# Layer 1 of a four-layer convolution stack: a 3x3 convolution computed by pairs of rows

## The chip, the cores and the metric

The kernel runs on one core of a Trainium2 chip. The metric is the device time of one execution in microseconds; the time before is the median of three runs. A profile is one further execution, recorded by the hardware profiler. TensorE (PE) multiplies matrices and writes to PSUM, VectorE (DVE) and ScalarE (ACT) work element by element on SBUF and PSUM, GpSimd (POOL) here clears borders and issues the stores, and SyncE (SP) issues the loads. Each engine works through its own list of instructions in order and waits on semaphores for the others.

## What is computed

The input x has the shape (4, 64, 256, 256): four images (batches) of 64 channels, all in float32. Four layers follow one another, each of the form x = x + f(groupnorm(x)), with 32 groups of two channels. Cut to what matters here:

```python
x = x + _L0_conv_ref(_gn(x), ...)      # 1x1, 8x8 patch filter, depthwise 3x3, gelu gate, 1x1
x = x + _L1_conv_ref(_gn(x), kernel)   # this layer
x = x + _L2_conv_ref(_gn(x), ...)      # masked periphery
x = x + _L3_conv_ref(_gn(x), ...)      # spectral layer

def _L1_conv_ref(x, kernel):           # kernel: (64, 64, 3, 3)
    return jax.lax.conv_general_dilated(x, kernel, window_strides=(1, 1),
        padding=[(1, 1), (1, 1)], dimension_numbers=('NCHW', 'OIHW', 'NCHW'))
```

So layer 1 is a dense 3x3 convolution from 64 to 64 channels with a border of zeros, on the normalized input, and the input itself is added to the result (the residual).

## The kernel before

The four layers run one after the other; each keeps its result in DRAM (`x1`, `x2`, `x3`), and the next reads it. Layers 0 and 2 write out the order of the instructions on PE, DVE, ACT and SP by hand (`tc.manual_schedule`); layer 1 before the change leaves the order to the scheduler of the language, which follows the data dependencies and the order of the program text.

Layer 1 (`_layer1`, from L703) works in 64 steps: for each of the 4 batches 16 steps of 16 image rows. In a step the upper 8 rows lie on partitions 0 to 63 (one channel each) and the lower 8 rows on partitions 64 to 127. `halves` are these two ranges.

- `load(n)` fetches a step, one step ahead: the tile `x` with 10 rows per half (8 and one on either side, L724), and, in another arrangement, the tile `xr` with the same 8 rows per half once more (L728). `xr` serves as residual and takes the result.
- `normalize` (L210, called at L748) is one ScalarE instruction that scales and shifts `x` by the group norm's values of the batch and writes `xn`, which is two columns wider; GpSimd clears those two columns (L737), and the outer row at the top and bottom of an image.
- The products are at L755. For two values of `i` (a pair of output rows in each block of four) and the nine taps `k` of the kernel, four matmuls of 64x64 weights with 2 x 256 columns are issued: `s` says which half of the partitions is read, `j` which of two blocks of four rows, and the result of block `j` lands in the half `j` of a PSUM tile `ps[s]`. The nine taps are accumulated in PSUM. That makes 2 x 9 x 4 = 72 matmuls a step. An fp32 matmul leaves two records in the trace.
- For each of the two PSUM tiles VectorE adds the residual (L761) and takes the statistics that the next group norm needs (L762, `bn_stats`).
- GpSimd issues two stores to `x2` (L765).
- After the last step of a batch `group_norm` (L149, its steps at L153 to L175) aggregates the statistics (L158) and turns them into scale and shift of layer 2: two small matmuls (L161, L170), small VectorE operations and a power on GpSimd (L174).

Layer 2 begins by loading its constants on SP (`load`, L138), then its first tiles of `x2` (L832). VectorE operations of other layers that serve below as a price: L454 (layer 0, a product of an SBUF and a PSUM tile of 1024 elements), L968 (layer 2, an addition of two SBUF tiles of 1024 elements), L980 (layer 2, statistics of 512 elements) and, for ScalarE, L950 (layer 2, a copy of 1024 elements from PSUM).

Of the kernel before, what the change touches and what calls it, by code (L numbers as in the profile page):

```python
# [10 lines left out]
F32 = mybir.dt.float32  # L11
U32 = mybir.dt.uint32
AF = mybir.ActivationFunctionType
ALU = mybir.AluOpType
PSUM = bass.MemoryType.PSUM
DRAM = bass.MemoryType.DRAM

C = 64
# [96 lines left out]
class _Net:  # L115
# [93 lines left out]
    def normalize(self, dst, src, n, b, p0=0, p1=128):  # L209
        self.nc.scalar.activation(  # L210
            dst, src, AF.Identity, bias=self.nb[n][p0:p1, b : b + 1], scale=self.r[n][p0:p1, b : b + 1]
        )
# [483 lines left out]

    def layer1(self, src, dst):
        with ExitStack() as ctx:  # L700
            self._layer1(ctx, src, dst)

    def _layer1(self, ctx, src, dst):  # L703
        tc, nc, a, B, H, W = self.tc, self.nc, self.a, self.B, self.H, self.W
        pool = lambda name, bufs, **k: ctx.enter_context(tc.tile_pool(name=name, bufs=bufs, **k))
        cp, p_x, p_n, p_r = pool("l1c", 1), pool("l1x", 3), pool("l1n", 2), pool("l1r", 3)
        ps_o, ps_s = pool("l1po", 6, space=PSUM), pool("l1ps", 1, space=PSUM)
        small = lambda name: ps_s.tile([128, 512], F32, tag="s", name=name)
        W1 = W + 1
        wk = cp.tile([128, 9, C], F32, name="wk")  # L710
        for s in range(2):
            nc.sync.dma_start(wk[s * C : (s + 1) * C], a["k3"].rearrange("c y x o -> c (y x) o"))
        its = [(b, r0) for b in range(B) for r0 in range(0, H, 16)]
        halves = [slice(0, C), slice(C, 128)]
        tiles = [(s, j) for s in range(2) for j in range(2)]
        raws = {}

        def load(n):
            b, r0 = its[n]
            x = p_x.tile([128, 10, W], F32, tag="x", name=f"x1_{n}")  # L720
            for s in range(2):
                top = r0 + 8 * s - 1
                i0, i1 = max(0, -top), min(10, H - top)
                nc.sync.dma_start(x[halves[s], i0:i1], src[b][:, top + i0 : top + i1, :])  # L724
            xr = p_r.tile([128, 2, 4, W], F32, tag="xr", name=f"xr1_{n}")
            v = src[b][:, r0 : r0 + 16, :].rearrange("c (s j r) w -> j c s r w", s=2, j=2)
            for j in range(2):
                nc.sync.dma_start(xr[halves[j]], v[j])  # L728
            raws[n] = x, xr

        load(0)
        for n, (b, r0) in enumerate(its):
            if n + 1 < len(its):
                load(n + 1)
            x, xr = raws.pop(n)
            xn = p_n.tile([128, 10, W + 2], F32, tag="xn", name=f"xn1_{n}")
            nc.gpsimd.memset(xn[:, :, 0 : W + 2 : W + 1], 0.0)  # L737
            i0, i1 = 0, 10
            if r0 == 0:
                i0 = 1  # L740
                nc.gpsimd.memset(xn[0:C, 0, 1:W1], 0.0)
                self.normalize(xn[C:128, 0, 1:W1], x[C:128, 0], 1, b, C, 128)
                bst = self.stats_tile(f"bst2_{b}", H * W // 1024)
            if r0 + 16 == H:
                i1 = 9
                nc.gpsimd.memset(xn[C:128, 9, 1:W1], 0.0)
                self.normalize(xn[0:C, 9, 1:W1], x[0:C, 9], 1, b, 0, C)
            self.normalize(xn[:, i0:i1, 1:W1], x[:, i0:i1], 1, b)  # L748
            for i in range(0, 4, 2):
                ps = [ps_o.tile([128, 2, W], F32, tag="o", name=f"ps1_{n}_{i}_{s}") for s in range(2)]  # L750
                for k in range(9):
                    dy, dx = divmod(k, 3)
                    for s, j in tiles:
                        r = 4 * j + i + dy
                        nc.tensor.matmul(  # L755
                            ps[s][halves[j]], wk[halves[s], k, :], xn[halves[s], r : r + 2, dx : dx + W],
                            start=(k == 0), stop=(k == 8),
                        )
                for s in range(2):
                    xo = xr[:, s, i : i + 2]  # L760
                    nc.vector.tensor_add(xo, xo, ps[s])  # L761
                    nc.vector.bn_stats(bst[:, r0 // 4 + i + s, :], xo.rearrange("p r w -> p (r w)"))  # L762
            v = dst[b][:, r0 : r0 + 16, :].rearrange("c (s j r) w -> j c s r w", s=2, j=2)
            for j in range(2):
                nc.gpsimd.dma_start(v[j], xr[halves[j]])  # L765
            if r0 + 16 == H:
                self.group_norm(2, b, bst, small)

# [497 lines left out]
```

## Time and profile before

| what | before |
|---|---|
| median of three runs | 7874.6 us |
| the three runs | 7872.5, 7874.6, 7885.55 us |
| the profiled execution | 7916.6 us |
| its span, first to last instruction | 7914.8 us |
| PE busy | 7529.5 us (95%) |
| DVE busy | 6190.4 us (78%) |
| ACT busy | 3598.1 us (45%) |
| POOL busy | 644.5 us (8%) |
| mean granted TensorE clock | 0.969 |
| layer 1, first to last product (4917.3 to 5931.9 us) | 1014.6 us |
| PE, DVE and ACT busy in that stretch | 1005.4, 347.0, 161.4 us |
| DMA share and rate in that stretch | 0.82, 209 GB/s |

A row of the groups gives line, engine, operation, output and inputs with their shapes and the count, then the total busy time in us with the mean time of one in ns, then the time that the engine stood idle just ahead of such instructions and which engine's work ended the wait. Busy times are unions: four matmuls that run at the same time in different parts of the array count once. The windows give busy times of PE, weight loads (PEld), DVE, ACT and POOL in a stretch, with the clock granted to TensorE (1.00 is full speed) and the load on the DMA engines.

### The profile page before, as it was taken

Reading aid. Unit: us, or ns where it says so; the run is one execution under the profiler, and the core shown is the slowest. Engines: PE = TensorE matmul, PEld = TensorE weight load, DVE = VectorE, ACT = ScalarE, POOL = GpSimd, SP = SyncE. Lnnn points to the kernel's source line nnn. Section 1 sums busy time; section 2 is a strip of 40 time slices with the busy share of each in tenths; the row PEclk is TensorE's granted clock in tenths of the full one; section 3 lists DMA queues with packets and bytes.
Section 4 is the critical chain, followed back from the end, with each engine's and each line's share of the span. In section 5 each row is a group of like instructions: output and inputs, shape, how many; then the busy total and the mean of one; then the engine's idle time right before and its main releaser. Section 6 shows DMA issues by size and latency. Waiting matters only on the chain.

```text
span 7914.8 us, 402431 instructions
## 1 busy us (share of the span) xinstructions
PE 7529.5 (95%) x191350; PEld 4403.3 (56%) x191350; DVE 6190.4 (78%) x5653; ACT 3598.1 (45%) x3853; POOL 644.5 (8%) x1465
## 2 busy tenths in 40 slices
PE   5999999999999999999999998999998999997887
PEld 3666666666666666666666665333333444443375
DVE  6999999999999999999989987333337889885345
ACT  2444444444544444444444453111117778774111
POOL 0000000000000000000000000000001222221000
PEclk9999999999999999999999999999999999999955
DMA  5222222222222222221112113888876666667679
GB/s 118 63 61 64 65 58 61 61 60 60 62 60 59 60 62 58 60 61 48 45 45 49 45 48 88 220 214 211 213 185 164 174 176 176 174 175 234 234 301 390
DMA packets 520862, 942.83 MB, mean 119 GB/s; under 512 B 44996, under 2 KB 308116, under 8 KB 501812
## 3 DMA queue, kind: packets, MB, share of 16 engines
q1 hardware_dynamic: 438708, 648.59, 29.9%
q0 software_dynamic: 80512, 268.50, 12.4%
q8 instruction: 1500, 24.58, 1.4%
q14 instruction: 142, 1.16, 0.1%
HBM read 648.48 MB, written 268.44 MB: 116 GB/s over the span
## 4 chain that ended last, share of the span: by engine, by line
PE 88%; DMA 4%; DVE 4%; issue 2%; ACT 1%; SPq 0%; DVEq 0%; ACTq 0%; POOLq 0%; POOL 0%
PE psd L434 30%; PE ps L755 13%; PE psy L407 10%; PE psu L369 8%; PE one L938 7%; PE div L897 5%; PE pso L509 3%; DMA x<-x 3%; PE psz L927 2%; PE psa L1112 2%; PE psF L356 2%; DVE v L472 2%; PE psT L346 2%; PE pso L500 1%; DMA st<-in_x_dram 1%
## 5 line engine op out<-in xcount | busy, mean ns | idle before, releaser
L434 PE MATMUL psd<-y,diag 32*32 32x512 f32 x73296 | 2539.2, 597 | 9.0 <-issue 7.9
L472 DVE SCALAR_TENSOR_TENSOR v<-y,sb_w_dw,v 128x2048 f32<-128x2048 f32 x1024 | 2391.0, 2335 | 108.7 <-ACT v L470 85.9
L434 PEld LDWEIGHTS psd<-y,diag 32*32 32x32 f32 x73296 | 1525.3, 103 | 860.0 <-issue 341.3
L414 ACT COPY y<-psy 128x512 f32<-128x512 f32 x1536 | 915.7, 660 | 1704.4 <-PE psy L407 1702.6
L372 DVE TENSOR_TENSOR up<-psu,flt 128x768 f32<-128x768 f32 x1024 | 932.5, 951 | 238.8 <-PE psu L369 237.8
L407 PEld LDWEIGHTS psy<-sb_c_bdft,up 64*64 64x64 f32 x49152 | 861.3, 135 | 353.2 <-issue 141.9
L755 PE MATMUL ps<-xn,wk 64*64 64x512 f32 x9216 | 1002.8, 592 | 9.7 <-ACT xn L210 9.7
L407 PE MATMUL psy<-sb_c_bdft,up 64*64 64x64 f32 x49152 | 933.1, 221 | 36.5 <-issue 33.7
L210 ACT ACTIVATE xn<-x,nb,r 128x1024 f32<-128x1024 f32 (+3 forms) x272 | 487.8, 1797 | 898.7 <-POOL xn L737 809.7
L369 PE MATMUL psu<-win,xf 64*64 64x384 f32 x8192 | 791.1, 487 | 20.5 <-DVE h L454 10.0
L755 PEld LDWEIGHTS ps<-xn,wk 64*64 64x64 f32 x9216 | 348.8, 133 | 655.3 <-issue 655.2
L761 DVE TENSOR_TENSOR xr<-xr,ps 128x512 f32<-128x512 f32 x256 | 173.7, 679 | 657.8 <-PE ps L755 657.8
L883 DVE TENSOR_TENSOR q<-xn 128x2313 f32<-128x2313 f32 (+2 forms) x256 | 627.7, 2496 | 13.6 <-ACT xn L210 13.6
L938 PE MATMUL one<-z,wp 32*32 32x512 f32 x16384 | 594.4, 596 | 14.0 <-issue 12.1
L884 ACT ACTIVATE q<-q 128x2313 f32<-128x2313 f32 (+2 forms) x256 | 529.0, 2086 | 30.5 <-DVE q L883 29.1
L938 PEld LDWEIGHTS one<-z,wp 32*32 32x32 f32 x16384 | 371.9, 103 | 216.1 <-issue 79.1
L448 ACT ACTIVATE h<-psd 128x1024 f32<-128x1024 f32 x258 | 250.8, 1022 | 527.6 <-PE psd L434 527.5
L897 PE MATMUL div<-q,ones 64*32 64x512 f32 x8192 | 462.8, 596 | 11.4 <-ACT q L884 9.8
L369 PEld LDWEIGHTS psu<-win,xf 64*64 64x64 f32 x8192 | 311.1, 134 | 184.0 <-issue 83.2
L379 POOL MEMSET y<- 128x22 f32 x384 | 51.7, 136 | 4261.3 <-ACT y L387 3225.5
L971 POOL DMA_DIRECT2D x<-r x512 | 271.9, 538 | 978.9 <-DVE r L968 953.4
L897 PEld LDWEIGHTS div<-q,ones 64*32 64x32 f32 x8192 | 152.7, 107 | 314.1 <-issue 244.4
(121 smaller groups left out, 6628.5 us busy)
## 6 DMA issues: line engine op xcount, KB each, us to landing
x<-x SPq DMA_DIRECT2D x240, 640.0 KB, 6.7
x<-x SPq DMA_DIRECT2D x61, 2048.0 KB, 13.4
st<-in_x_dram SPq DMA_DIRECT2D x256, 256.0 KB, 3.6
x<-in_x_dram SPq DMA_DIRECT2D x256, 256.0 KB, 3.8
xr<-x SPq DMA_DIRECT2D x128, 512.0 KB, 5.3
x<-xr POOLq DMA_DIRECT2D x128, 512.0 KB, 6.4
r<-x SPq DMA_DIRECT2D x512, 128.0 KB, 4.1
x<-r POOLq DMA_DIRECT2D x512, 128.0 KB, 4.0
```

What stands on the lines that cost most here:

```text
L210: self.nc.scalar.activation(dst, src, AF.Identity, bias=self.nb[n][p0:p1, b : b + 1], scale=self.r[n][p0:p1, b : b + 1])
L369: nc.tensor.matmul(ps[halves[n], s, 0:384], xf[t][halves[s], n, 4 * g + k], win[halves[s]], start=True, stop=True)
L372: nc.vector.tensor_mul(ups[t, g][:, :, k, :], ps[:, :, 0:384], flt.broadcast_to([128, 2, 384]))
L407: nc.tensor.matmul(ps[halves[c], n, s, :, k, :], up[halves[n], s, k, i * 128 + c * C : i * 128 + (c + 1) * C], bdft[halves[n]], start=True ...
L414: nc.scalar.copy(yt[t][i][:, 3:11, w0 : w0 + 64].rearrange("p r (k n w) -> p n r k w", k=4, n=2), ps[:, :, s])
L434: ins = nc.tensor.matmul(d[q // 2][quarters[j], q % 2], diag[quarters[q], i, k, :], rows_in(t, i, quarters[q], j, dy)[:, :, dx : dx + W], ...
L472: nc.vector.scalar_tensor_tensor(v, s, wdw[:, 2, k : k + 1], v, ALU.mult, ALU.add)
L755: nc.tensor.matmul(ps[s][halves[j]], wk[halves[s], k, :], xn[halves[s], r : r + 2, dx : dx + W], start=(k == 0), stop=(k == 8),)
L883: nc.vector.tensor_sub(d, p0, p1)
L884: nc.scalar.activation(d, d, AF.Square)
L897: ins = nc.tensor.matmul(ps[quarters[j], h], ones[halves[h]], q[n, g, k][halves[h], r + 2 * j : r + 2 * j + 2, o : o + W], start=(m == 0), ...
L938: ins = nc.tensor.matmul(rows2(ps[g])[quarters[j], k], w[quarters[i]], z[quarters[i], h, 2 * j + dy : 2 * j + dy + 2, dx : dx + W], tile_p ...
```

## The change

The convolution is computed by pairs of output rows. For input rows d0 to d3 (normalized, with border) and the three rows w0, w1, w2 of the kernel, a pair of output rows needs d0 w0 + d1 w1 + d2 w2 and d1 w0 + d2 w1 + d3 w2. With the weights g1 = (w0 + w1 + w2) / 2 and g2 = (w0 - w1 + w2) / 2 and the four products

- m0 = (d0 - d2) w0, m1 = (d1 + d2) g1, m2 = (d2 - d1) g2, m3 = (d3 - d1) w2

the pair is m0 + m1 + m2 and m1 - m2 + m3. Each product stands for its three horizontal taps, accumulated in PSUM. The rows of a step form four such pairs per half. So there are 4 x 3 = 12 tap products over all pairs where 2 x 9 = 18 were needed.

The combinations of rows are made by VectorE (`transform`, four instructions of 4 x 258 elements a step). Of the four PSUM tiles (128 x 1024 elements each) m1 is copied to SBUF by ScalarE (`fetch`), m1 + m2 and m1 - m2 are made by VectorE (`middle`), and VectorE adds m0 to the one and m3 to the other (`result`), into a new tile `o`. The residual is accumulated into m0 and m3 by a further product of the raw tile `x` with an identity matrix, so the tile `xr` and its two loads go. Statistics and stores work on `o`. The order on PE, DVE, ACT and SP is now written by hand; loads run three steps ahead, the normalization two, and the steps of the group norm are spread over the following steps of the loop (`next_norms`). The lines of the diff, without the unchanged ends of functions (`load`'s and `normalize`'s bodies stay as they are but for the buffers):

```diff
-        cp, p_x, p_n, p_r = pool("l1c", 1), pool("l1x", 3), pool("l1n", 2), pool("l1r", 3)
-        ps_o, ps_s = pool("l1po", 6, space=PSUM), pool("l1ps", 1, space=PSUM)
+        cp, p_x, p_n, p_t = pool("l1c", 1), pool("l1x", 4), pool("l1n", 1), pool("l1t", 2)
+        p_s, p_o, pp = pool("l1s", 2), pool("l1o", 3), pool("l1p", 1, space=PSUM)
+        def pair(name):
+            return pp.tile([128, 2, 512], F32, tag=f"p{next(turn) % 4}", name=name)
...
+        gs = [wk[:, 0]] + [cp.tile([128, 3, C], F32, name=f"wg{k}") for k in range(2)] + [wk[:, 2]]
+        side = cp.tile([128, 3, C], F32, name="wside")
+        nc.vector.tensor_add(side, wk[:, 0], wk[:, 2])
+        for g, op in ((gs[1], nc.vector.tensor_add), (gs[2], nc.vector.tensor_sub)):
+            op(g, side, wk[:, 1])
+            nc.vector.tensor_scalar(g, g, 0.5, None, ALU.mult)
+        xns = [p_n.tile([128, 10, W + 2], F32, name=f"xn1_{k}") for k in range(2)]
+        for t in xns:
+            nc.gpsimd.memset(t[:, :, 0 : W + 2 : W1], 0.0)
...
-            xr = p_r.tile([128, 2, 4, W], F32, tag="xr", name=f"xr1_{n}")
-            v = src[b][:, r0 : r0 + 16, :].rearrange("c (s j r) w -> j c s r w", s=2, j=2)
-            for j in range(2):
-                nc.sync.dma_start(xr[halves[j]], v[j])
...
-            for i in range(0, 4, 2):
-                ps = [ps_o.tile([128, 2, W], F32, tag="o", name=f"ps1_{n}_{i}_{s}") for s in range(2)]
-                for k in range(9):
-                    dy, dx = divmod(k, 3)
-                    for s, j in tiles:
-                        r = 4 * j + i + dy
-                        nc.tensor.matmul(
-                            ps[s][halves[j]], wk[halves[s], k, :], xn[halves[s], r : r + 2, dx : dx + W],
-                            start=(k == 0), stop=(k == 8),
-                        )
-                for s in range(2):
-                    xo = xr[:, s, i : i + 2]
-                    nc.vector.tensor_add(xo, xo, ps[s])
-                    nc.vector.bn_stats(bst[:, r0 // 4 + i + s, :], xo.rearrange("p r w -> p (r w)"))
...
+        def transform(n, *which):
+            xn = xns[n % 2]
+            if n not in ts:
+                ts[n] = p_t.tile([128, 4, 4, W + 2], F32, tag="t", name=f"t_{n}")
+            d = [xn[:, k : k + 7 : 2] for k in range(4)]
+            for i in which:
+                p, q, op = (
+                    (d[0], d[2], nc.vector.tensor_sub),
+                    (d[1], d[2], nc.vector.tensor_add),
+                    (d[2], d[1], nc.vector.tensor_sub),
+                    (d[3], d[1], nc.vector.tensor_sub),
+                )[i]
+                op(ts[n][:, i], p, q)
+
+        def product(n, i):
+            m = ms[n, i] = pair(f"m{i}_{n}")
+            tiles = [(s, j) for s in range(2) for j in range(2)]
+            for dx in range(3):
+                for s, j in tiles:
+                    nc.tensor.matmul(
+                        rows2(m)[halves[j], s], gs[i][halves[s], dx, :],
+                        ts[n][halves[s], i, 2 * j : 2 * j + 2, dx : dx + W],
+                        start=(dx == 0), stop=(dx == 2 and i in (1, 2)),
+                    )
+            if i in (0, 3):
+                r = 1 if i == 0 else 2
+                for s, j in tiles:
+                    nc.tensor.matmul(
+                        rows2(m)[halves[j], s], self.ident[halves[s], halves[s]],
+                        xt[n][halves[s], r + 4 * j : r + 4 * j + 3 : 2], start=False, stop=True,
+                    )
+
+        def fetch(n):
+            t = sums[n, 1] = p_s.tile([128, 2, 512], F32, tag="s1", name=f"s1_{n}")
+            nc.scalar.copy(t, ms.pop((n, 1)))
+
+        def middle(n):
+            m1, m2 = sums.pop((n, 1)), ms.pop((n, 2))
+            for i, op in ((0, nc.vector.tensor_add), (3, nc.vector.tensor_sub)):
+                t = sums[n, i] = p_s.tile([128, 2, 512], F32, tag=f"s{i}", name=f"s{i}_{n}")
+                op(t, m1, m2)
+
+        def result(n, i):
+            if n not in outs:
+                outs[n] = p_o.tile([128, 2, 4, W], F32, tag="o", name=f"o1_{n}")
+            r = i // 3
+            nc.vector.tensor_add(
+                outs[n][:, :, r : r + 3 : 2], rows2(ms.pop((n, i))), rows2(sums.pop((n, i)))
+            )
+
+        def finish(n):
+            o = outs.pop(n)
+            for s in range(2):
+                for i in (0, 2):
+                    nc.vector.bn_stats(bst[b][:, r0 // 4 + i + s, :], o[:, s, i : i + 2].rearrange("p r w -> p (r w)"))
+            v = dst[b][:, r0 : r0 + 16, :].rearrange("c (s j r) w -> j c s r w", s=2, j=2)
+            for j in range(2):
+                nc.gpsimd.dma_start(v[j], o[halves[j]])
+            if r0 + 16 == H:
+                norms.append(self.group_norm_parts(2, b, bst.pop(b), lambda name: pair(name)[:, 0, :]))
...
+            for n in range(3):
+                load(n)
+            for n in range(2):
+                normalize(n)
+            transform(0, 1, 2, 0, 3)
+            for n in range(NI):
+                load(n + 3)
+                product(n, 1)
+                fetch(n)
+                product(n, 2)
+                finish(n - 1)
+                transform(n + 1, 1, 2)
+                middle(n)
+                product(n, 0)
+                result(n, 0)
+                transform(n + 1, 0, 3)
+                normalize(n + 2)
+                product(n, 3)
+                result(n, 3)
+                next_norms()
+                xt.pop(n)
+                ts.pop(n)
+            finish(NI - 1)
+            while norms:
+                next_norms()
```

More of the change, by code (lines that the diff above doesn't have):

```diff
@@ L705, in _layer1 @@
         pool = lambda name, bufs, **k: ctx.enter_context(tc.tile_pool(name=name, bufs=bufs, **k))
-        cp, p_x, p_n, p_r = pool("l1c", 1), pool("l1x", 3), pool("l1n", 2), pool("l1r", 3)
-        ps_o, ps_s = pool("l1po", 6, space=PSUM), pool("l1ps", 1, space=PSUM)
-        small = lambda name: ps_s.tile([128, 512], F32, tag="s", name=name)
+        cp, p_x, p_n, p_t = pool("l1c", 1), pool("l1x", 4), pool("l1n", 1), pool("l1t", 2)
+        p_s, p_o, pp = pool("l1s", 2), pool("l1o", 3), pool("l1p", 1, space=PSUM)
+        turn = count()
+        def pair(name):
+            return pp.tile([128, 2, 512], F32, tag=f"p{next(turn) % 4}", name=name)
+        rows2 = lambda t: t.rearrange("p s (r w) -> p s r w", r=2)
         W1 = W + 1
-        wk = cp.tile([128, 9, C], F32, name="wk")
+        halves = [slice(0, C), slice(C, 128)]
+        wk = cp.tile([128, 3, 3, C], F32, name="wk")
         for s in range(2):
-            nc.sync.dma_start(wk[s * C : (s + 1) * C], a["k3"].rearrange("c y x o -> c (y x) o"))
+            nc.sync.dma_start(wk[halves[s]], a["k3"])
+        gs = [wk[:, 0]] + [cp.tile([128, 3, C], F32, name=f"wg{k}") for k in range(2)] + [wk[:, 2]]
[7 more added lines that the diff above has]
+            nc.gpsimd.memset(t[:, :, 0 : W + 2 : W1], 0.0)
         its = [(b, r0) for b in range(B) for r0 in range(0, H, 16)]
-        halves = [slice(0, C), slice(C, 128)]
-        tiles = [(s, j) for s in range(2) for j in range(2)]
-        raws = {}
+        NI = len(its)
+        xt, ts, ms, sums, outs, bst, norms = {}, {}, {}, {}, {}, {}, []
         def load(n):
+            if n >= NI:
+                return
             b, r0 = its[n]
-            x = p_x.tile([128, 10, W], F32, tag="x", name=f"x1_{n}")
+            x = xt[n] = p_x.tile([128, 10, W], F32, tag="x", name=f"x1_{n}")
             for s in range(2):
@@ L724, in load, with normalize @@
                 nc.sync.dma_start(x[halves[s], i0:i1], src[b][:, top + i0 : top + i1, :])
-            xr = p_r.tile([128, 2, 4, W], F32, tag="xr", name=f"xr1_{n}")
-            v = src[b][:, r0 : r0 + 16, :].rearrange("c (s j r) w -> j c s r w", s=2, j=2)
-            for j in range(2):
-                nc.sync.dma_start(xr[halves[j]], v[j])
[L729 to L737, printed above, removed]
+        def normalize(n):
+            if n >= NI:
+                return
+            b, r0 = its[n]
+            x, xn = xt[n], xns[n % 2]
             i0, i1 = 0, 10
@@ L742, in _layer1 @@
                 self.normalize(xn[C:128, 0, 1:W1], x[C:128, 0], 1, b, C, 128)
-                bst = self.stats_tile(f"bst2_{b}", H * W // 1024)
             if r0 + 16 == H:
@@ L748, in _layer1 @@
             self.normalize(xn[:, i0:i1, 1:W1], x[:, i0:i1], 1, b)
-            for i in range(0, 4, 2):
-                ps = [ps_o.tile([128, 2, W], F32, tag="o", name=f"ps1_{n}_{i}_{s}") for s in range(2)]
-                for k in range(9):
-                    dy, dx = divmod(k, 3)
-                    for s, j in tiles:
-                        r = 4 * j + i + dy
-                        nc.tensor.matmul(
-                            ps[s][halves[j]], wk[halves[s], k, :], xn[halves[s], r : r + 2, dx : dx + W],
-                            start=(k == 0), stop=(k == 8),
-                        )
-                for s in range(2):
-                    xo = xr[:, s, i : i + 2]
-                    nc.vector.tensor_add(xo, xo, ps[s])
-                    nc.vector.bn_stats(bst[:, r0 // 4 + i + s, :], xo.rearrange("p r w -> p (r w)"))
+        def transform(n, *which):
+            if n >= NI:
+                return
+            xn = xns[n % 2]
[10 more added lines that the diff above has]
+                op(ts[n][:, i], p, q)
@@ L763, in _layer1 @@
+        def finish(n):
+            if n < 0:
+                return
+            b, r0 = its[n]
+            if b not in bst:
+                bst[b] = self.stats_tile(f"bst2_{b}", H * W // 1024)
+            o = outs.pop(n)
+            for s in range(2):
+                for i in (0, 2):
+                    nc.vector.bn_stats(bst[b][:, r0 // 4 + i + s, :], o[:, s, i : i + 2].rearrange("p r w -> p (r w)"))
             v = dst[b][:, r0 : r0 + 16, :].rearrange("c (s j r) w -> j c s r w", s=2, j=2)
@@ L764, in _layer1, with next_norms @@
             for j in range(2):
-                nc.gpsimd.dma_start(v[j], xr[halves[j]])
+                nc.gpsimd.dma_start(v[j], o[halves[j]])
             if r0 + 16 == H:
-                self.group_norm(2, b, bst, small)
+                norms.append(self.group_norm_parts(2, b, bst.pop(b), lambda name: pair(name)[:, 0, :]))
+        def next_norms():
+            for parts in list(norms):
+                if next(parts, self) is self:
+                    norms.remove(parts)
+        with tc.manual_schedule(
+            engines={
+                mybir.EngineType.PE, mybir.EngineType.DVE, mybir.EngineType.Activation, mybir.EngineType.SP
+            }
+        ):
+            for n in range(3):
[23 more added lines that the diff above has]
+                next_norms()
```

## The prediction

> **What bounds the kernel now.** I read the page's slices first, since the change lies in one layer and a share over the whole span mixes four.
>
> ```profile
> PE   5999999999999999999999998999998999997887
> DVE  6999999999999999999989987333337889885345
> PEclk9999999999999999999999999999999999999955
> DMA  5222222222222222221112113888876666667679
> ```
>
> A slice is 197.9 us. Slices 26 to 30 are layer 1: TensorE full, VectorE at three tenths, the DMA engines at eight. Next the groups of instructions there, and the rows that price the new operations (line, engine, operation, names, shapes, count | busy us, mean ns | idle before it and what ended that).
>
> ```profile
> L755 PE MATMUL ps<-xn,wk 64*64 64x512 f32 x9216 | 1002.8, 592 | 9.7 <-ACT xn L210 9.7
> L761 DVE TENSOR_TENSOR xr<-xr,ps 128x512 f32<-128x512 f32 x256 | 173.7, 679 | 657.8 <-PE ps L755 657.8
> L762 DVE BATCH_NORM_STATS2 bst<-xr 128x6 f32<-128x512 f32 x256 | 177.7, 694 | 8.8
> L968 DVE TENSOR_TENSOR r<-r,sel 128x1024 f32<-128x1024 f32 x128 | 151.3, 1228 | 2.7 <-DMA r<-x 2.7
> L454 DVE TENSOR_TENSOR h<-h,psd 128x1024 f32<-128x1024 f32 x256 | 300.1, 1213 | 2.2 <-PE psd L434 1.8
> L950 ACT COPY sel<-zero 128x1024 f32<-128x1024 f32 x128 | 122.3, 1009 | 9.9 <-PE zero L938 9.9
> ```
>
> VectorE idles 657.8 us waiting for TensorE; TensorE idles 9.7 us. Layer 1 is bound by TensorE. Then the chain of waits in order of time, at the first change of batch, and two windows (busy us and count of each engine, granted TensorE clock, DMA share, GB/s): one undisturbed, one at that change.
>
> ```profile
> 4917.33 249.94 PE ps L755 x2238
> 5167.29 0.70 DVE xr L761
> ...
> 5170.06 1.90 DVE mv L158
> 5172.00 0.58 PE gn L161 x2
> 5172.59 1.90 PE ps L755 x4
> 5174.48 0.52 PE gv L170 x2
> 5175.00 247.39 PE ps L755 x2287
> ```
> ```profile
> 5200.00:5400.00 200.00, 200.00 (x1872) 67.38 (x1864) 68.33 (x104) 33.10 (x14) 17.22 (x40) 1.00 0.84 220
> 5167.00:5177.00 10.00, 6.95 (x34) 2.51 (x30) 5.40 (x10) 2.52 (x1) 1.87 (x4) 0.73 0.94 248
> ```
>
> The reader is to see that products run without a gap at full clock, except where the statistics of a batch end: there TensorE stands 3.05 us for L158, and four records after it take 1.90 us. By the timeline VectorE takes the half-tiles every 7.73 us in steady state (5915.68, 5923.40, 5931.13), and across the first change of batch 15.62 us (5167.29 to 5182.91), so a change costs 15.62 - 7.73 = 7.9 us.
>
> [...] the clock is 0.50 in the pause before layer 1 (4901 to 4917) and 0.73 around the 3.05 us gap. [...] a record (an fp32 matmul leaves two: 9216 for 4608) lasts 592 ns, yet 1872 fit into 200 us. [...]
>
> **The change, part by part.** There are 4 x 16 = 64 steps of 16 rows.
>
> 1. Products. Before, a step has 2 x 9 x 4 = 72 matmuls in 18 groups of four that run together, and takes 2 x 7.73 = 15.45 us, so a group costs 0.858 us. After, four products of three groups, and two of them get a fourth group, the identity one: 14 groups, same 64x512 shape, same four array positions, 12.02 us. Per step -3.43 us, times 64 = **-219.6 us**, all on the bounding engine.
> 2. Changes of batch. The three norms inside the layer are now spread over three steps: L158's aggregation is queued a full step ahead of the matmul that needs it. The 7.9 us become two small matmul pairs of 0.58 and 0.52 us: 3 x (7.9 - 1.1) = **-20.4 us**.
> 3. Head. Layer 1's first load starts where it did (4905.21; it waits for layer 0's last store), its data land at 4914.3, ScalarE is done at 4917.3. Now one combination (1.24 us) lies between that and the first product: **+1.2 us**. Half clock at the start costs 68 records in 9.67 us instead of 90, about 2.4 us, before and after alike. [...]
> 4. Tail. Layer 2's constant loads are queued on SP behind the last use of `wk`; before, that was the last matmul (SP starts at 5931.98, TensorE ends at 5931.9), after it one identity group follows: **-0.9 us**. Layer 2's loads of batch 0 need batch 0's stores, long landed. The last store and norm of layer 1 come about 2 us later than now after the last product, beside layer 2's 10 us of loading.
> 5. VectorE. Per step: four statistics at 0.694 = 2.78; four combinations of 1032 elements, the 1228 of L968 plus 8 elements, 1.236 each = 4.94; two `middle` and two `result` with one PSUM operand, 1.213 each = 4.85. Sum 12.57 us, which is above TensorE's 12.02. But independent neighbours overlap: six statistics of L980 in one piece of the timeline take 3.66 us against 6 x 0.686 = 4.12, two of L968 2.37 against 2.46: 0.09 per neighbour. Eleven of the twelve have such a neighbour: 12.57 - 1.0 = **11.6 us**, 97% of TensorE's step. So it costs nothing if the cover holds; if it doesn't, up to 0.55 us x 64 = 35 us.
> 6. Waits that are new. In steady state each of a step's four products waits for something VectorE or ScalarE did earlier. Counting from the start of a step, products 1, 2, 0, 3 end at 2.6, 5.2, 8.6, 12.0. VectorE: `result` 3 of the step before until 1.4, statistics to 3.9, two combinations to 6.2, `middle` to 8.5, `result` 0 after product 0, 8.7 to 9.9, two combinations to 12.2. Next step's product 2 needs `middle` at 14.6, its product 0 needs its combination (11.1) at 17.2: 6 us to spare. A norm adds to VectorE 1.89 (L158), small operations and the wait for POOL's power (0.68 before), some 4 us in three steps, less than the 6; it is made good at 0.4 us a step. Behind VectorE's waiting instruction stand the statistics and the next combinations, behind TensorE's the next products. Whether a satisfied wait costs TensorE anything is not shown at this density: the group of L755 has 68 semaphore instructions of 51 ns in 64 steps, and no loss. Ends: 0, and 3 per step x 51 ns x 64 = 10 us; I take 3.
> 7. ScalarE: `fetch` 1.01 and normalize 2.5 of 12 us; its fetch ends 1 us after product 1, before product 2 does. DMA: the second read of x (2 x 512 KB) goes; a step moves 1.25 MB in and 1 MB out where it moved 3.25 MB. At 0.84 busy for 15.45 us that is 13.0 us for 3.25 MB, so 9 us for 2.25 MB, inside 12. Loads are queued on SP three steps ahead and wait for the buffer of the step before. POOL issues two stores a step as before (1.19 us) and loses a memset. None of it is late.
>
> Sum: -219.6 - 20.4 + 1.2 - 0.9 + 3 = -236.7 us, made against the profiled execution: span 7914.8, 7916.6 with what lies around it. That execution is 42.0 us (0.5%) above the median of 7874.6; I take the same microseconds off the median: 7874.6 - 236.7, about **7638 us**.
>
> **The rivals.**
> - VectorE becomes the bound. For: it is within 3% of TensorE's step even with the overlap. Against: the overlap shows in every dense piece of the trace, across waits too. Without it, 64 x 12.57 = 804 us plus 4 us for each of three norms = 816 instead of TensorE's 775: +41, that is 7679. Half the overlap: 12.1 us, about 7655.
> - The hand-overs are exposed. PSUM is taken in turn by four tiles, and four products per step go to and fro between engines; if 1 us a step stays on TensorE, 64 us: 7702. Against: step 6 finds 6 us of room.
> - Slower than before. One mechanism: VectorE stretches the step so far that TensorE stands 3 us in each, and its clock halves as it did after the 3.05 us gap. Then a step's products take up to 24 us, and steps settle between, say 18: 64 x 18 = 1152 against 1014.6, 8012 us. It loses from 1014.6 / 64 = 15.85 us a step; the clock starts to fall at 12.0 + 3.05 = 15.1. VectorE's twelve operations would have to cost 25% more than their rows; layer 1's denser transfers speak for it (DMA 0.84, where L968's layer 2 has 0.65), its own L761 at 679, no slower than 512 elements should be beside L454's 1024, against.
> - The change doesn't do what it says: the built program has the 56 matmuls per step in the order written, and no second load. Only a hidden cost at the start or end of the layer is left, and a little better is possible too: 7625.
>
> **How the numbers follow.** TensorE-bound, 7638: 0.63. VectorE-bound, 7655 to 7683: 0.22. Hand-overs, about 7702: 0.08. A little better than the sum, 7622 to 7630: 0.03. Slower: 0.04. The range takes in the first two whole and the fourth: 7622 to 7690. A measurement here tells 0.2% (16 us) from none: faster 0.95, same 0.01, slower 0.04.
>
> **What would show it.** Right: in an undisturbed 200 us of layer 1 TensorE stays at 200 busy and clock 1.00 with the same 1870 records, VectorE at about 190; products start to start 12.0 us a step; no TensorE gap at the changes of batch; layer 1's products span 775 us. Wrong: TensorE idle ended by VectorE, a step of 12.5 us or more, combinations well over 1.24 us, a clock under 1, or another stretch of the kernel longer than before.

## The result and the profile after

| what | before | after |
|---|---|---|
| median of four runs of each | 7880.1 us | 7650.7 us |
| range of the runs | 7872.5 to 7887.6 us | 7643.8 to 7661.1 us |
| the profiled execution | 7916.6 us | 7654.2 us |
| its span | 7914.8 us | 7652.4 us |
| layer 1, first product to last | 4917.3 to 5931.9, 1014.6 us | 4895.0 to 5669.0, 774.0 us |
| DVE busy | 6190.4 us (78%) | 6594.1 us (86%) |
| mean granted TensorE clock | 0.969 | 0.968 |

The kernel became faster: the ratio is 0.971 with a 95% interval of 0.9693 to 0.9727. That is 229.4 us less, between 215 and 242 by the interval. The forecast was 236.7 us less, 7638 us. The time before is now the median of four runs, 7880.1 us; with the three above it was 7874.6 us.

First the slices of the page of the changed kernel. A slice is 191.3 us now.

```profile
PE   5999999999999999999999999899989999997887
DVE  6999999999999999999999999899979989884345
PEclk9999999999999999999999999999999999999955
DMA  5222222222222222222111211477766666666689
```

The stretch with VectorE at three tenths is gone: in slices 27 to 29, wholly layer 1, TensorE and VectorE both stand at nine tenths, and in the two beside them, which it shares with layers 0 and 2, at eight or seven and more. The DMA engines are at seven where they were at eight. Next the groups of layer 1, forms kept apart, from 4860 us on for TensorE and ScalarE and from 4917 us on for VectorE (which so misses the first step or two).

```profile
L786 PE MATMUL m<-t,wk 64*64 64x512 f32 x3072 | 352.7, 588 | 0.0
L786 PE MATMUL m<-t,wg 64*64 64x512 f32 x3072 | 343.4, 591 | 11.0 <-DVE t L779 11.0
L794 PE MATMUL m<-x,sb_c_ident 64*64 64x512 f32 x1024 | 132.9, 589 | 0.0
L801 ACT COPY s<-m 128x1024 f32<-128x1024 f32 x64 | 64.8, 1013 | 542.5 <-PE m L786 542.5
```
```profile
L779 DVE TENSOR_TENSOR t<-xn 128x1032 f32<-128x1032 f32 x246 | 290.6, 1223 | 0.0
L826 DVE BATCH_NORM_STATS2 bst<-o 128x6 f32<-128x512 f32 x252 | 155.5, 680 | 1.8
L813 DVE TENSOR_TENSOR o<-m,s 128x1024 f32<-128x1024 f32 x126 | 153.9, 1221 | 14.7 <-PE m L794 14.7
L807 DVE TENSOR_TENSOR s<-s,m 128x1024 f32<-128x1024 f32 x125 | 146.5, 1213 | 1.5 <-PE m L786 1.5
```

TensorE's 9216 records have become 3072 + 3072 + 1024 = 7168, each as long as before (588 to 591 ns). It waits 11.0 us in the whole layer, all of it ahead of the very first product (the first combination, L779). The 657.8 us that VectorE waited for TensorE are down to some 16 (14.7 and 1.5). Then two windows, the first undisturbed, the second over the first change of batch, and the chain of waits across that change.

```profile
5200.00:5400.00 200.00, 200.00 (x1864) 71.29 (x1860) 194.93 (x206) 59.23 (x36) 21.19 (x37) 1.00 0.74 197
5085.00:5135.00 50.00, 50.00 (x468) 18.09 (x463) 47.83 (x54) 13.74 (x8) 5.28 (x9) 1.00 0.73 200
```
```profile
5101.35 7.72 PE m L786 x72
5109.08 0.86 PE m L794 x8
5109.93 2.58 PE m L786 x24
5112.51 0.86 PE m L794 x8
5113.37 0.31 PE gn L161 x2
5113.68 7.88 PE m L786 x72
...
5125.86 0.31 PE gv L170 x2
5126.17 7.88 PE m L786 x72
```

TensorE is busy 50.00 of 50 us at full clock where it stood 3.05 us before. A step there takes 12.33 (5101.35 to 5113.68) and 12.49 us (5113.68 to 5126.17) against 12.02 elsewhere.

**Where the 262.4 us between the two spans lie.** Four stretches, cut at TensorE's products:

| stretch | before | after | difference |
|---|---|---|---|
| layer 0, to the end of its last product | 4901.0 | 4877.4 | -23.6 |
| from there to layer 1's first product | 16.3 | 17.6 | +1.3 |
| layer 1's products | 1014.6 | 774.0 | -240.6 |
| from there to layer 2's first product | 18.8 | 18.2 | -0.6 |
| the rest | 1964.1 | 1965.2 | +1.1 |

The 23.6 us of layer 0 are not the change's. Its instructions are the same; the profiled execution before was 36.5 us above its median, the one after 3.5 us, and in two runs below (experiments 2 and 3), with the same layer 0, layer 1's first product starts at 4896.90 and at 4880.95 us. What belongs to the change is -240.6 + 1.3 - 0.6 = -239.9 us, within what the runs give.

### The profile page after: what moved, and what is told of

It is laid out like the page before. It is cut to its first block, busy times and chain, and to the rows that moved or that the text cites. A ratio compares the mean times of both kernels' runs of the same rounds, so it can differ in the third digit from the quotient of the medians.

```text
span 7652.4 us, 398676 instructions
## 1 busy us (share of the span) xinstructions
PE 7291.6 (95%) x189302; PEld 4324.6 (57%) x189302; DVE 6594.1 (86%) x5914; ACT 3656.9 (48%) x3917; POOL 637.7 (8%) x1403
## 4 chain that ended last, share of the span: by engine, by line
PE 88%; DVE 4%; DMA 4%; issue 2%; ACT 1%; SPq 0%; DVEq 0%; ACTq 0%; POOLq 0%; POOL 0%
PE psd L434 31%; PE psy L407 10%; PE m L786 9%; PE psu L369 9%; PE one L1038 7%; PE div L997 5%; PE pso L509 3%; DMA x<-x 3%; DVE v L472 2%; PE psz L1027 2%; PE psa L1212 2%; PE psF L356 2%; PE psT L346 2%; PE m L794 1%; PE pso L500 1%
## 5 line engine op out<-in xcount | busy, mean ns | idle before, releaser
L997 PE MATMUL div<-q,ones 64*32 64x512 f32 x8192 | 465.1, 596 | 10.3 <-ACT q L984 9.3
L786 PE MATMUL m<-t,wg 64*64 64x512 f32 x3072 | 343.4, 591 | 11.0 <-DVE t L779 11.0
L786 PE MATMUL m<-t,wk 64*64 64x512 f32 x3072 | 352.7, 588 | 0.0
L801 ACT COPY s<-m 128x1024 f32<-128x1024 f32 x64 | 64.8, 1013 | 542.5 <-PE m L786 542.5
```

The lines of the kernel that those rows point to most:

```text
L786: nc.tensor.matmul(rows2(m)[halves[j], s], gs[i][halves[s], dx, :], ts[n][halves[s], i, 2 * j : 2 * j + 2, dx : dx + W], start=(dx == 0), ...
L997: ins = nc.tensor.matmul(ps[quarters[j], h], ones[halves[h]], q[n, g, k][halves[h], r + 2 * j : r + 2 * j + 2, o : o + W], start=(m == 0), ...
```

## The experiments

The theory was that layer 1 is bound by TensorE's 14 groups a step, with VectorE just beneath and the hand-overs hidden. Each kernel below changes one part of the kernel that its paragraph names. "Step" is the time between two equal instructions one step apart in steady state, "products" the stretch from layer 1's first product to its last. The runs fall on three chips, with medians of 7879.1, 7833.0 and 7855.0 us for the kernel before; across them ratios and stretches are compared, not medians.

**1. The order alone (`e1_order_only`).** The kernel before, its 18 groups and both loads kept, with the order written by hand, the normalization a step ahead and the norms spread as in the changed kernel:

```diff
-            if r0 + 16 == H:
-                self.group_norm(2, b, bst, small)
...
+                if r0 + 16 == H:
+                    norms.append(self.group_norm_parts(2, b, bst.pop(b), small))
+                next_norms()
```

> The kernel before with one part of the change alone: its 18 tap products per step, its two loads and its additions stay, but the order on PE, DVE, ACT and SP is written by hand, the normalization runs one step ahead and the steps of a batch's norm are spread over the following steps. My theory (TensorE bounds layer 1; of the gain about 220 us are products left out and about 20 us the three changes of batch): the step stays at 15.45 us, the gap of TensorE at the changes of batch goes, layer 1's products span about 994 us instead of 1014.6, the whole about 20 us less than before (7858). Rival (the gain comes from the hand-written order, which hides waits inside the step): well over 20 us less, the step under 15.4 us.

Measured: 7859.3 us against 7879.1, ratio 0.9977 (0.9968 to 0.9985), products 995.0 us. The order, with the norms spread, is worth 1014.6 - 995.0 = 19.6 us, the 20.4 of the forecast. The chain at its first change of batch has no wait left, and half a step (72 records) takes 7.73 us as before, so nothing was gained inside the step:

```profile
5149.87 7.73 PE ps L775 x72
5157.59 0.31 PE gn L161 x2
5157.91 15.61 PE ps L775 x144
5173.52 0.31 PE gv L170 x2
```

**2. Without the residual (`e2_no_identity`).** The two identity groups go; the output lacks the residual of layer 1.

```diff
-                        start=(dx == 0), stop=(dx == 2 and i in (1, 2)),
-                    )
-            if i in (0, 3):
...
-                        xt[n][halves[s], r + 4 * j : r + 4 * j + 3 : 2], start=False, stop=True,
+                        start=(dx == 0), stop=(dx == 2),
```

> The changed kernel without its identity products, so that the residual of layer 1 is left out: 12 groups of products a step instead of 14. Theory: TensorE's step would be 10.3 us, but VectorE is right behind with 11.7 us (194.9 busy in 200 us), so the step falls only to about 11.7 us, layer 1's products span 750 to 765 us where the changed kernel has 773.4, the whole is 8 to 23 us less than the changed kernel, and TensorE idles about 1.4 us a step for VectorE. Rival (TensorE alone decides, VectorE has room): 64 x 1.72 = 110 us less, a step of 10.3 us.

Measured: 7621.6 us, ratio 0.967 (0.9648 to 0.9692), products 747.2 us, 26.8 less than the changed kernel, a little more than the 8 to 23 expected. Had TensorE still been the bound, two groups of 0.858 us in 64 steps would have given 110 less. The window and two VectorE instructions one step apart:

```profile
5200.00:5400.00 200.00, 184.53 (x1636) 69.59 (x1636) 198.00 (x210) 60.06 (x36) 21.20 (x37) 0.98 0.78 199
```
```profile
5203.11 1.21 DVE L806 TENSOR_TENSOR o<-m,s 128x1024 f32<-128x1024 f32 x1
5214.71 1.22 DVE L806 TENSOR_TENSOR o<-m,s 128x1024 f32<-128x1024 f32 x1
```

VectorE is now the bound (198.00 of 200), and its twelve instructions take 11.60 us a step. That is the number that the forecast had worked out as 12.57 less the overlap. So the changed kernel stands 0.42 us a step above VectorE's bound.

**3. The second read of x put back (`e3_second_load`).** The changed kernel, with the loads of `xr` that it had saved, their data unused.

```diff
+            xr = p_r.tile([128, 2, 4, W], F32, tag="xr", name=f"xr1_{n}")
+            v = src[b][:, r0 : r0 + 16, :].rearrange("c (s j r) w -> j c s r w", s=2, j=2)
+            for j in range(2):
+                nc.sync.dma_start(xr[halves[j]], v[j])
```

> The changed kernel with the second read of x put back (two loads of 512 KB a step into a tile that nobody reads). Theory: before, the DMA engines were 0.84 busy over 15.45 us, 13.0 us a step for 3.25 MB; at that rate a step of 12.0 us has no room for them, transfers become the bound and the step grows to about 13 us: about 60 us more than the changed kernel, layer 1 about 835 us, DMA share close to 1. Rival (transfers are hidden either way, leaving out the second read was worth nothing): the step stays at 12.0 us, layer 1 at 773 us, DMA share about 0.95 or less.

Measured: 7649.0 us, ratio 0.9709 (0.9685 to 0.9734), products 775.1 us. No loss; the theory was wrong here.

```profile
5200.00:5400.00 200.00, 200.00 (x1867) 71.17 (x1860) 194.65 (x206) 59.23 (x36) 20.21 (x36) 1.00 0.98 282
```

The DMA engines move 282 GB/s at a share of 0.98, and TensorE does not wait. The kernel before had 220 GB/s at 0.84, from which a full share would be 262. A busy share times the step is therefore not the time that the transfers need. Leaving out the second read was worth nothing that can be measured; the kernel gains from the products and the order.

**4. One more VectorE instruction a step (`e4_one_more_vector_op`).** A fifth combination of 1032 elements, its result unused.

```diff
+            if 3 in which:
+                nc.vector.tensor_sub(spare, d[3], d[0])
```

> The changed kernel with a fifth combination of rows a step on VectorE (1032 elements, 1.22 us, overlapped 1.14), whose result nobody reads. Theory (VectorE is 0.3 us short of being the bound): VectorE's step becomes 12.85 us and decides; layer 1 grows by 64 x 0.83 = 53 us and by some 4 us for each of three norms, which TensorE no longer hides: 50 to 68 us more than the changed kernel. Rival 1 (VectorE has more room than its busy time says, since neighbours overlap): under 15 us more. Rival 2 (once TensorE pauses, its clock falls): over 150 us more, clock in the stretch under 0.9.

Measured: 7693.3 us, ratio 0.9763 (0.9741 to 0.9784), products 821.6 us, 47.6 more than the changed kernel, just under the 50 to 68 expected. Two `result` one step apart:

```profile
5199.79 1.22 DVE L816 TENSOR_TENSOR o<-m,s 128x1024 f32<-128x1024 f32 x1
5212.53 1.22 DVE L816 TENSOR_TENSOR o<-m,s 128x1024 f32<-128x1024 f32 x1
```

The step is 12.74 us, 1.14 more than the 11.60 of twelve instructions; 64 x (12.74 - 12.02) = 46. The cover of the changed kernel is 0.42 us a step and what exceeds it is paid in full. The clock does not collapse: 0.98 in 5200 to 5400.

**5 and 6. Four more, in one place and spread.** To see whether TensorE's waits feed themselves, as the rival on the slower side had it, the changed kernel was given four additional combinations a step: in `e8_four_more_in_one_place` all behind the last two combinations, in `e9_four_more_spread` one in each of four places. Their results are unused. The lines are those of the first; the second calls `extra(n + 1, 1)` in its four places.

```diff
+        def extra(n, count):
+            if n >= NI:
+                return
+            for k in range(count):
+                nc.vector.tensor_sub(spare, xns[n % 2][:, 3:10:2], xns[n % 2][:, 0:7:2])
...
+            if 3 in which:
+                extra(n, 4)
```

> The changed kernel with four more VectorE combinations a step (1032 elements, result unused) in one place, behind the last two combinations. Question: the prediction's slower rival, that a stand of TensorE of 3 us and more in each step halves its clock and the loss feeds itself. My theory: VectorE alone sets the step. The kernel with one more had 12.74 us against 11.60 for twelve instructions, so 1.14 us each: 12.74 + 3 x 1.14 = 16.16 us a step, products of layer 1 821.6 + 64 x 3.42 = 1040 us, the whole about 7912 us. TensorE stands some 4.1 us a step, and even if its clock falls for a while the products it then runs slowly are taken from that stand. Rival (the one on record): steps settle at 18 us with a clock well under 1, the stretch at 1152 us, the whole at 8024.

> The same four additional VectorE combinations a step, but one in each of four places: ahead of the first two combinations, behind `middle`, ahead of and behind the last two combinations. My theory: the same sum on VectorE, the same 16.16 us a step and 7912 us, within 0.2% of the kernel with all four in one place; TensorE's stand is cut in more pieces, so the granted clock is no lower than there. Rival: the place matters; with all four in one place TensorE stands longest at a time, its clock falls, and that kernel is slower than this one by over 0.5% (40 us).

Measured, against 7855.0 us of the kernel before on this chip: all in one place 7911.6 us, ratio 1.0077 (1.0062 to 1.0092), products 1064.2 us; spread 7879.6 us, ratio 1.0035 (1.0023 to 1.0048), products 1035.1 us, its step 16.18 us (5203.13 to 5219.31). The spread kernel hits VectorE's sum (1040 forecast). The other has 29 us more in the products, and 32 us (0.4%) more in all: more than the 0.2% that my theory allowed, less than the rival's 0.5%, and far from its 1152 us. TensorE's timelines, first all in one place, then spread (start, length, records; in brackets the wait before it and for whom):

```profile
5104.22 5.40 PE L795 MATMUL m<-t,wk 64*64 64x512 f32 x24 [3.17 <-DVE o L822]
...
5120.77 2.81 PE L795 MATMUL m<-t,wk 64*64 64x512 f32 x24 [1.44 <-DVE o L822]
...
5306.30 2.81 PE L795 MATMUL m<-t,wk 64*64 64x512 f32 x24 [2.60 <-DVE o L822]
...
5322.85 2.81 PE L795 MATMUL m<-t,wk 64*64 64x512 f32 x24 [3.17 <-DVE o L822]
```
```profile
5110.74 2.81 PE L793 MATMUL m<-t,wg 64*64 64x512 f32 x24 [1.11 <-DVE t L786]
...
5118.71 2.81 PE L793 MATMUL m<-t,wk 64*64 64x512 f32 x24 [1.76 <-DVE t L786]
```

With all four in one place the clock does fall: behind the first stand of 3.17 us the next 24 records take 5.40 us instead of 2.81, and the clock granted from 5103.20 to 5110.03 was 0.50. Another stand of 3.17 us and one of 2.60 leave the records at 2.81. Spread, the stands of an undisturbed step are 1.76 us and shorter, and all records stay at 2.81. Mean clocks in 5200 to 5400 are 0.92 and 1.00. Stands down to 2.60 us brought the fall (at 4938.76, with 4.50 us for the next 24 records), though not each time.

But the fall does not cost the 29 us. With slow records the step is 16.55 us (5104.22 to 5120.77), and without any it is 16.55 us as well (5306.30 to 5322.85): the slow records only shorten TensorE's next stand, from 3.17 to 1.44 us. The step is VectorE's, and VectorE's own list is longer here. Its timelines, in one place and spread:

```profile
5316.63 5.02 DVE L770 TENSOR_TENSOR spare<-xn 128x1032 f32<-128x1032 f32 x4
5321.57 1.22 DVE L822 TENSOR_TENSOR o<-m,s 128x1024 f32<-128x1024 f32 x1
```
```profile
5216.80 1.23 DVE L770 TENSOR_TENSOR spare<-xn 128x1032 f32<-128x1032 f32 x1
5217.94 2.37 DVE L786 TENSOR_TENSOR t<-xn 128x1032 f32<-128x1032 f32 x2
```

In one place the four take 5321.57 - 5316.63 = 4.94 us of VectorE's time, spread 1.14 us each, 4.56 in all. That is the 0.37 us between the two steps (16.55 and 16.18), about 23 of the 29 us; most of the rest lies in the first step and the last. Within the group of four the second to the fourth begin 0.03 us after the one ahead has ended, where neighbours elsewhere begin 0.08 us before. All four write the same tile, each right behind the other; whether that is the reason is not shown, as no run here gives them tiles of their own. So the rival's mechanism exists, but it does not feed itself, and in the undisturbed step it costs nothing.

**7. The residual folded into the weights (`e5_fold_residual`).** Can the cover be turned into time? The input is (normalized - nb) / r with the group norm's scale r and shift nb, so a diagonal of 1/r in the middle tap, and -nb/r in ScalarE's copy, give the residual without the identity groups. TensorE has 12 groups again, with the whole result computed.

```diff
+                g = mids[b][i - 1] if dx == 1 and i in (1, 2) else gs[i][:, dx]
...
-            nc.scalar.copy(t, ms.pop((n, 1)))
+            nc.scalar.activation(t, ms.pop((n, 1)), AF.Identity, bias=shift[:, b : b + 1])
```

> The identity products replaced by nothing on TensorE: the residual is put into the weights. Since x = (xn - nb) / r, the diagonal of the middle tap gets 1/r of its input channel (a set of weights for each batch, made once at the start of the layer), and ScalarE's fetch adds the constant -nb/r on its way. 12 groups of products a step. Theory (VectorE's twelve operations, 11.60 us, are next, as in the run without identity products): a step of 11.60 us, 20 to 30 us less than the changed kernel, the new small operations hidden ahead of the first load's landing. Rival (more to gain: TensorE alone decides): 10.3 us a step, 110 us less. Third possibility (the constant on ScalarE or the start costs what is gained): within 8 us of the changed kernel.

Measured, against 7833.0 us of the kernel before on this chip: 7572.9 us, ratio 0.967 (0.9655 to 0.9684), products 749.0 us, step 11.6 us, VectorE 198.00 of 200. Like experiment 2, 25 us less than the changed kernel and no more, since VectorE holds it.

**8. One combination on GpSimd (`e6_fold_and_pool`).** Experiment 7, with the fourth combination off VectorE.

```diff
+                if i == 3:
+                    op = nc.gpsimd.tensor_sub
```

> As the kernel with the residual in the weights, and one of the four combinations of rows a step moved from VectorE to GpSimd. Theory (VectorE bounds the former): VectorE falls to 10.46 us, TensorE to 10.3; if GpSimd takes under 5 us for it and doesn't hold VectorE up, the step falls to about 10.5 us, 64 x 1.1 = 70 us less than the former. Rival (GpSimd and VectorE hinder each other at SBUF, or GpSimd is so slow that product 3 waits): no less than the former, perhaps more, with VectorE's other operations longer than 1.22 us.

Measured: 7518.1 us, ratio 0.9597 (0.9581 to 0.9613), products 691.6 us: 57.4 less than experiment 7 where 70 were expected. In the undisturbed step VectorE gains what was expected: two of its results are 10.46 us apart (5418.63 and 5429.09), 1.14 less than before. That is still 0.16 above TensorE's 10.30, so VectorE holds the step; TensorE's 100.00 busy of 100 us in 5400 to 5500 only show it catching up behind a change of batch. Most of what is missing is lost at these changes: one costs VectorE 7.0 to 7.7 us beyond the undisturbed steps, in experiment 7 it costs 3.5, and 5200 to 5400, with one in it, has TensorE at 188.07 of 200. VectorE's and GpSimd's timelines behind a change:

```profile
5400.67 0.16 DVE L175 SCALAR_TENSOR_TENSOR nb<-gm,r 128x1 f32<-128x1 f32 x1 [2.25 <-POOL r L174]
...
5407.66 1.22 DVE L826 TENSOR_TENSOR o<-m,s 128x1024 f32<-128x1024 f32 x1
5408.80 1.73 DVE L796 TENSOR_TENSOR t<-xn 128x1032 f32<-128x1032 f32 x1
5410.45 1.21 DVE L826 TENSOR_TENSOR o<-m,s 128x1024 f32<-128x1024 f32 x1
...
5418.63 1.22 DVE L826 TENSOR_TENSOR o<-m,s 128x1024 f32<-128x1024 f32 x1
...
5429.09 1.22 DVE L826 TENSOR_TENSOR o<-m,s 128x1024 f32<-128x1024 f32 x1
```
```profile
5407.06 2.38 POOL L796 TENSOR_TENSOR t<-xn 128x1032 f32<-128x1032 f32 x1 [5.82 <-PE m L805]
```

VectorE waits 2.25 us for POOL's power, which comes behind GpSimd's combination in its list (1.44 us in the changed kernel). And the combinations of the two collide. GpSimd works until 5407.06 + 2.38 = 5409.44. VectorE's combination begins at 5408.80 and ends at 5410.53, that is 1.09 us after GpSimd is done; the `result` before it, which reads one operand from PSUM, takes its usual 1.22 us beside GpSimd. The trace shows such a hold-up only in the first steps of the layer and around the changes of batch: 9 of VectorE's 192 combinations take over 1.3 us, the longest 3.43, the others the usual 1.22.

**9. The statistics on ScalarE (`e7_fold_and_scalar_stats`).** Experiment 7, with the four `bn_stats` a step replaced by a sum and a sum of squares that ScalarE accumulates; a few small operations a batch make mean and variance of them. The stores are issued later in the step.

```diff
+            nc.scalar.activation(
+                junk, outs[n].rearrange("p s r w -> p (s r w)"), (AF.Identity, AF.Square)[k],
+                accum_out=bst[b][:, k, r0 // 16 : r0 // 16 + 1],
+            )
```

> As the kernel with the residual in the weights, and the statistics of the result moved from VectorE to ScalarE: two passes of 2048 elements a step that accumulate the sum and the sum of squares (about 2.0 us each by L470's row), combined at the end of a batch. Theory: VectorE falls to 11.60 - 2.47 = 9.1 us, ScalarE rises to 3.6 + 4.2 = 7.8, TensorE's 12 groups decide with 12 x 0.858 = 10.3 us: 64 x 1.72 = 110 us less than the changed kernel, TensorE without gaps. Rival (ScalarE's longer list delays fetch, so that VectorE and then TensorE wait): a step of 11 us or more.

Measured: 7494.7 us, ratio 0.9567 (0.9553 to 0.9581), products 665.3 us, 108.7 less than the changed kernel. The window has TensorE full again:

```profile
5200.00:5400.00 200.00, 200.00 (x1862) 71.31 (x1858) 180.13 (x167) 141.69 (x118) 25.31 (x44) 1.00 0.91 227
```

With VectorE relieved, 12 groups run at TensorE's 12 x 0.858 = 10.3 us a step. This version beats both kernels: 1.5% under the changed one, by the ratios 0.9567 and 0.971.

## Why the prediction was right, step by step

1. Products: right. 64 steps of 12.02 us, with 0.858 us a group unchanged. Stretch forecast 775 us, measured 774.0; the first two steps of the sum, -219.6 - 20.4 = -240.0, measured -240.6.
2. Changes of batch: right, and shown alone by experiment 1 (-19.6 for -20.4). In the changed kernel one costs 12.33 + 12.49 - 2 x 12.02 = 0.8 us; 1.1 was forecast.
3. Head: right. From the first load's issue to the first product 13.31 us (4881.69 to 4895.00) against 12.12 before, +1.2 as forecast. The five operations on the weights ended at 4886.35, before ScalarE began on the first load's data at 4890.65.
4. Tail: -0.6 for -0.9.
5. VectorE: right, and it was the step that decided between the likeliest case and the first rival. The sum of rows, 12.57 us, would have been above TensorE's 12.02. Experiment 2 laid VectorE's step bare: 11.60 us. The rows of the changed kernel (four of 0.680 and of 1.223 us, two of 1.221 and of 1.213) sum to 12.48, so the overlap is 0.88; that the forecast's 12.57 - 1.0 came so close is in part luck, as its rows and its overlap were both some 0.1 us too large. In the trace most neighbours of this step overlap: two combinations take 2.37 us and not 2.45, and a thirteenth costs 1.14 us and not 1.22. The cover of 0.42 us a step was real, and so was its price: experiment 4 pays 47.6 us.
6. New waits: nothing instead of +3 us. TensorE's 200.00 busy of 200 leaves no room for a price of satisfied waits. The wait for POOL's power was 1.44 us (0.68 was taken), and with the aggregation (1.88) it was made good without a stand of TensorE.
7. Transfers: the outcome right, the method not. "At 0.84 busy for 15.45 us that is 13.0 us for 3.25 MB" treated the busy share as the time the transfers need. Experiment 3 moves the 3.25 MB in 12.02 us. The forecast was not hurt, as 2.25 MB had room by either reckoning.

Of the sum nothing but the 3 us of step 6 was off by over 1.5 us. The 7 us between 236.7 and the medians' 229.4 lie inside the interval of 215 to 242. The time itself is 12.7 us above the forecast of 7638, and 5.5 of them come from the median of before, which rose with the fourth run.

Of the rivals, VectorE as the bound was near: 0.42 us a step. Its price for half the overlap was mis-summed: in the way of the line before it, 64 x 12.1 + 12 = 786 us, that is 11 above 775 and 7649, not 7655. The slower rival was wrong in how it joined two true things. With four more combinations in one place TensorE does stand 3 us in a step and its clock does fall (0.50 behind a stand of 3.17 us), but the rival added the slow products to the step, up to 18 us. Experiments 5 and 6 show that as long as TensorE waits for VectorE in each step, the slow products come out of its wait: the step is VectorE's, 16.18 us spread and 16.55 in one place. "It loses from 15.85 us a step" holds for both: they are slower than the kernel before. The rival of exposed hand-overs was not tried by itself; TensorE's full windows leave nothing for it.

## What to carry to other kernels

When work is taken off the bounding engine and put on an idle one, sum the new engine's step from measured rows with the overlap of neighbours, and set it against the new step of the old bound: here 11.6 against 12.02, and the next 1.2 us instruction would have cost 48 us. Once both engines are nearly full, a further saving on one is worth only the distance to the other (27 us of 110 in experiment 2), and the rest comes when the second is relieved as well (experiment 9). Slow stretches of an engine that waits for another in each step come out of its wait (16.55 us a step with them and without), so look for the cost of a longer step in the list of the engine that it waits for. A saved transfer counts only if something waited for it, and a busy share does not tell that (0.98 in experiment 3, without a loss).

## What the runs showed of the hardware that was not expected

- The share of busy DMA engines is no measure of the room left: 0.74 at 197 GB/s, 0.84 at 220 and 0.98 at 282, with TensorE at 200.00 of 200 in all three.
- TensorE's clock fell behind some stands of 2.60 to 3.17 us (the next 24 records took 4.12 to 5.40 us), and not behind others as long (2.81 us). Where TensorE waited for VectorE in each step this cost nothing: 16.55 us a step with slow records and without.
- Four VectorE combinations in a row into one tile took 4.94 us, where the same four, apart from each other, took 1.14 us each.
- A combination of 1032 elements takes 2.38 us on GpSimd against 1.22 on VectorE, and holds up a VectorE combination that falls beside it (1.73 us, ending 1.09 us after GpSimd's).
- A ScalarE pass over 2048 elements with an accumulated sum takes 1.90 us, and reading the accumulator another 0.19.
